# Moving the inverses of norms, their scales and the sums of weights to other slots of the opening of a transformer block

## Chip, cores and metric

The kernel runs on one core of one Trainium2 chip. The metric is the device time of one execution in microseconds; the median of three timed runs is given. Lower is better.

## What is computed

A residual around one transformer block whose norms are conditioned on a vector t. Shapes: x is 4 x 1024 x 512 (four batches of 1024 tokens), t is 4 x 128, 16 heads of 32, hidden size 2048, all float32.

```python
def rmsnorm(x, t, gw, gb, bw, bb):
    g = (t @ gw.T + gb)[:, None, :]
    b = (t @ bw.T + bb)[:, None, :]
    inv_rms = rsqrt(mean(x * x, axis=-1, keepdims=True) + 1e-6)
    return g * x * inv_rms + b

def block(x, t, ...):
    x = x + attention(rmsnorm(x, t, g1w, g1b, b1w, b1b), Wq, Wk, Wv, Wo)
    n = rmsnorm(x, t, g2w, g2b, b2w, b2b)
    return x + (silu(n @ gate_w.T) * (n @ hid_w.T)) @ out_w.T

out = x + block(x, t)
```

The attention is the usual softmax(q k / sqrt(32)) v over the 1024 tokens of a batch, followed by Wo.

## The kernel before

Activations lie with the 512 features over 4 chunks of 128 partitions (C = 4) and the tokens along the free axis. The tokens are cut into 8 blocks of 512 (NBLK = 8), two per batch (QB = 2, called halves). One loop over slots g = 0 to 267 runs everything but the start and the end. In slot g the scores of step r = g are formed: 4 heads, 256 queries, 256 keys. Four steps (UN = 4) make one j, which is one group of 4 heads and 256 queries; eight j (GB = 8), that is 32 slots (BS = 32), make one block of 512 queries. A first slot is one with g % 4 == 0, a second slot one with g % 4 == 1, and so on.

The order of the instructions on TensorE (PE), VectorE (DVE), ScalarE (ACT) and GpSimd (POOL) is written out by hand: each engine runs its instructions in the order of the program, so a late instruction holds up all that stands behind it on its engine. Only the order of SyncE (SP), which issues most DMAs, is left to the framework.

What one slot g of the opening (g below FS = 60) does, in program order:

- scores(g) on PE into the one PSUM tile sc (L337), and in a first slot fold_sum on DVE (L425)
- shifted(g-5) on DVE: the maximum is taken off the raw scores (L390); in a second slot in two halves, since the shift of that j arrives then: parts_T (pt, L374), spread (sp, L113) on PE and two copies on ACT (L385)
- weighted(g-6) on PE (L403), which needs the exponential that ACT made in the slot before; its sum over keys goes by an accumulating DMA from POOL (L417)
- keep(g) on ACT: copies the scores from PSUM (L344)
- exponential(g-5) on ACT (L393), which needs shifted(g-5)
- a projection (project_kq, project_v or project_out) on PE from a queue of chains; its result is copied by ACT to a staging tile and stored to DRAM, or, for project_out, added on DVE (L471). In even slots a second one follows, whose copy comes in the next slot
- in a first slot sums on PE (L435, over the folded tile), the running maximum (L352) and the transposes of the maxima (mt, L358) with parts on DVE (L364 to L369); in the other slots two running maxima (L349)
- what is filed under halfway (by between), then divide, which in a third slot, and for the last j of a block in a first slot, inverts and normalizes an earlier j (L443, L452), then what is filed under ended (by after)

The projections of batches 1 to 3 need their normed inputs y. For each half-batch (b, half) a slot s4 is worked out: 6, 14, 22, 30, 38 and 46, always a third slot. The chunk is loaded in slot s4-7 (L256); norm_squares runs at the end of s4-5 and s4-4 (ACT L139, DVE L142 and L145); norm_root in s4-3 (one product and a square root on ACT, L150, with loads of the activation table); the inverse at the end of s4-2 (L746, 128x512); the four norm_scale in s4 (DVE L200), one for each chunk c; the norm_mod on ACT (L203) at the end of s4 for c = 0, 1 and of s4+1 for c = 2, 3. The projections that use it start at s4+6.

The feed-forward stage from slot 60 on multiplies 2x2 blocks with sums of weights. These sums are made in the opening by weight_sums, for f = 0 to 15: step 0 issues two loads of 256 KB on SP (L495), step 1 does four DVE operations on 128x256 (L501 to L504) and issues two stores (L506). Its four tiles and the staging tiles of the projections share the tag h with seven buffers. Step 1 of f is at the end of slot 3f+6: slots 6, 9, 12 and so on to 51.

At the end of slots 47 and 48 the squares of the first feed-forward norm, f0, are formed (L139, L142, L145), and its mean in slot 49.

Of the kernel before, what the change touches and what calls it, by code (L numbers as in the profile page):

```python
# [24 lines left out]
def tile_cond_transformer_block(  # L25
# [13 lines left out]
    nc = tc.nc  # L39
# [77 lines left out]
    y, wkq, wv, wo, kq, v = {}, {}, {}, {}, {}, {}  # L117
# [3 lines left out]
    state = {}  # L121
# [13 lines left out]
    def norm_squares(dst, tag: str, k: int):  # L135

        sq = [sb.tile([P, NB], F32, tag="t", name=f"sq{tag}_{2 * k + i}", bufs=2) for i in range(2)]
        for i in range(2):
            nc.scalar.activation(sq[i], dst[:, 2 * k + i, :], AF.Square)  # L139
        if k == 0:  # L140
            state[tag] = sb.tile([P, NB], F32, tag="tot", name=f"tot{tag}", bufs=1)
            nc.vector.tensor_tensor(state[tag], sq[0], sq[1], ALU.add)  # L142
        else:
            for t in sq:
                nc.vector.tensor_tensor(state[tag], state[tag], t, ALU.add)  # L145
# [53 lines left out]
    def norm_scale(dst, tag: str, c: int):  # L199
        nc.vector.tensor_tensor(dst[:, c, :], dst[:, c, :], state[tag], ALU.mult)  # L200

    def norm_mod(which: int, b: int, dst, c: int):
        nc.scalar.activation(  # L203
            dst[:, c, :],
            dst[:, c, :],
            AF.Identity,
            bias=mod[:, (2 * which + 1) * C + c, b : b + 1],
            scale=mod[:, 2 * which * C + c, b : b + 1],
        )
# [498 lines left out]
    def pin(g, fn, *a):  # L708
        pinned.setdefault(g, []).append((fn, a))

    def between(g, fn, *a):
        halfway.setdefault(g, []).append((fn, a))

    def after(g, fn, *a):
        ended.setdefault(g, []).append((fn, a))

    def chains_of(b: int, half: int):
        todo = []
        for hg in range(C):
            todo.append(((load_wkq, (hg,)), project_kq, (b, hg, 0, half)))  # L720
            todo.append((None, project_kq, (b, hg, 1, half)))
        for kt in range(half * KT // 2, (half + 1) * KT // 2):
            todo.append((None, project_v, (b, kt)))
        return todo

    def enqueue(g: int, load, fn, a):
        queue.append((g, load, fn, a))
# [9 lines left out]
    for b in range(1, B):  # L737
        for half in range(QB):
            s = math.ceil((len(queue) + 1) / PACE)
            s4 = s - 4 - (s - 6) % UN  # L740
            tag = f"a{b}_{half}"
            pin(max(s4 - 7, 0), load_y, b, half)
            for k in range(2):
                after(s4 - 5 + k, lambda b=b, half=half, tag=tag, k=k: norm_squares(y[b, half], tag, k))
            between(s4 - 3, norm_root, tag)
            after(s4 - 2, lambda tag=tag: nc.vector.reciprocal(state[tag], state[tag]))  # L746
            for c in range(C):
                between(s4, lambda b=b, half=half, tag=tag, c=c: norm_scale(y[b, half], tag, c))
                after(s4 + c // 2, lambda b=b, half=half, c=c: norm_mod(0, b, y[b, half], c))
            for load, fn, a in chains_of(b, half):  # L750
                enqueue(s, load, fn, a)
    FS = BS + 28
    for f in range(NF):
        after(3 * f + 4, weight_sums, f, 0)
        after(3 * f + 6, weight_sums, f, 1)
    for n in range(NBLK):
        g0 = (n + 1) * BS
        pin(g0 + 6, load_res, n)
# [5 lines left out]
        if n < NBLK - 1:  # L764
            tag = f"f{n}"
# [46 lines left out]
    with tc.manual_schedule(  # L812
# [51 lines left out]
        g = 0  # L864
# [309 lines left out]
```

## Time and profile before

| what | us |
| --- | --- |
| median of three timed runs (2425.57 to 2426.95) | 2425.66 |
| the profiled execution | 2425.87 |
| its span, first to last instruction | 2424.1 |
| busy in the span: PE | 2374.3 |
| busy in the span: DVE | 1975.1 |
| busy in the span: ACT | 1420.1 |
| busy in the span: POOL | 172.4 |
| start, 0 to 44.49 | 44.49 |
| opening, slots 0 to 59 | 476.55 |
| attention and feed-forward, 521.04 to 2143 | 1621.96 |
| the rest of the feed-forward | 281.10 |

The mean granted clock of TensorE is 0.998. A row of the timeline gives the start and the duration in us, the engine, the line of the kernel, the operation, the tiles (written from read), the shapes and how many were merged; a bracket at its end is the time that the engine stood idle just before, and who released it. PE's ends are modelled, and successive rows overlap by about 0.1 us, so a cost in a chain is read from the start of one row to the start of the next.

The six long inverses take this much each (minimum, median and maximum in ns, then the first and last start):

```profile
L746 DVE RECIPROCAL tota<-tota x6: 3344/3346/3346, 79.7 to 402.6; 128x512 f32<-128x512 f32 x6
```

### The profile page before, as it was taken

How to read it: one execution, taken by the hardware profiler on the slowest of the kernel's cores; microseconds unless marked ns; L12 is line 12 of the kernel's file. 1: busy time of each engine (PE TensorE's matmuls, PEld its weight loads, DVE VectorE, ACT ScalarE, POOL GpSimd, SP SyncE). 2: the span in 40 equal slices, each digit the busy share in tenths (PEclk: the TensorE clock that was granted, in tenths of full speed). 3: DMA queues.
4: the chain of work that ended last, by engine and by line, in shares of the span. 5: the costliest groups of instructions: out<-in, count | busy, mean ns of one | idle time of the engine just before them, and what ended most of it. 6: DMA issues, size and time to landing. Idle time of an engine off the chain costs nothing. (4 is left out here: it accounts for less than half of the span.)

```text
span 2424.1 us, 74021 instructions
## 1 busy us (share of the span) xinstructions
PE 2374.3 (98%) x33149; PEld 1153.2 (48%) x33149; DVE 1975.1 (81%) x2295; ACT 1420.1 (59%) x1519; POOL 172.4 (7%) x207
## 2 busy tenths in 40 slices
PE   9999999999999999999999999999999999989999
PEld 4333434345454544544454545454545454434665
DVE  2688888889799988998899979997999799835544
ACT  4677776766566656665576657665666576412111
POOL 0000000000000000000000000000000000000000
PEclk9999999999999999999999999999999999999999
DMA  6699999889888888889888888898887988862331
GB/s 226 188 295 254 262 251 241 222 220 239 199 203 212 204 226 199 216 212 229 196 211 217 221 201 213 202 238 202 206 210 197 231 197 219 209 213 82 126 106 53
DMA packets 184843, 499.79 MB, mean 206 GB/s; under 512 B 21191, under 2 KB 78535, under 8 KB 157134
## 3 DMA queue, kind: packets, MB, share of 16 engines
q0 software_dynamic: 28656, 208.68, 44.4%
q1 hardware_dynamic: 155582, 286.37, 35.0%
q8 instruction: 261, 4.28, 0.7%
q14 instruction: 56, 0.46, 0.1%
q10 hardware_dynamic: 288, 0.01, 0.0%
HBM read 244.34 MB, written 41.97 MB: 118 GB/s over the span
## 5 line engine op out<-in xcount | busy, mean ns | idle before, releaser
L390 DVE TENSOR_TENSOR raw<-raw,shift 128x2048 f32<-128x2048 f32 (+1 forms) x320 | 588.8, 1857 | 26.1 <-ACT shift L385 26.1
L344 ACT COPY raw<-sc 128x2048 f32<-128x2048 f32 x256 | 479.4, 1873 | 186.2 <-PE sc L337 127.8
L393 ACT ACTIVATE raw<-raw 128x2048 f32<-128x2048 f32 x256 | 490.7, 1917 | 147.5 <-DVE raw L390 145.3
L349 DVE TENSOR_TENSOR rmax<-rmax,raw 128x1024 f32<-128x1024 f32 x384 | 469.5, 1223 | 47.6 <-ACT raw L344 41.0
L113 PE MATMUL pc<-h,ow 128*32 128x512 f32 x3328 | 379.9, 595 | 2.5 <-ACT raw L393 1.5
L417 POOL DMA_DIRECT2D raw<-raw x192 | 165.3, 861 | 1940.7 <-ACT raw L393 839.0
L337 PE MATMUL sc<-q,k 32*128 32x256 f32 x4096 | 293.3, 400 | 0.8 <-ACT raw L344 0.8
L403 PE MATMUL av<-raw,v 128*32 128x256 f32 x4096 | 272.5, 384 | 21.3 <-ACT raw L393 20.8
L113 PE MATMUL pa<-x,fa 128*32 128x256 f32 x4096 | 270.0, 381 | 3.5 <-DVE pa L551 2.5
L113 PE MATMUL pa<-sums,fw 128*32 128x256 f32 x4096 | 267.9, 379 | 0.0
L337 PEld LDWEIGHTS sc<-q,k 32*128 32x128 f32 x4096 | 185.0, 184 | 117.1 <-issue 74.9
L113 PE MATMUL pkq<-y,wkq 128*32 128x512 f32 (+1 forms) x1664 | 230.8, 596 | 0.9 <-ACT y L203 0.7
L113 PEld LDWEIGHTS pc<-h,ow 128*32 128x32 f32 x3328 | 103.7, 110 | 206.9 <-issue 193.0
L113 PEld LDWEIGHTS pa<-x,fa 128*32 128x32 f32 x4096 | 123.3, 110 | 112.1 <-DVE pa L551 20.9
L113 PEld LDWEIGHTS pa<-sums,fw 128*32 128x32 f32 x4096 | 133.1, 110 | 87.9
L403 PEld LDWEIGHTS av<-raw,v 128*32 128x32 f32 x4096 | 110.6, 109 | 134.5 <-ACT raw L393 48.7
L113 PE MATMUL pb<-x,fw 128*32 128x256 f32 x2048 | 134.7, 379 | 1.2 <-ACT pb L566 1.2
L113 PE MATMUL pa<-x,fw 128*32 128x256 f32 x2048 | 134.0, 379 | 0.0
L113 PE MATMUL pb<-sums,fa 128*32 128x256 f32 x2048 | 133.9, 379 | 0.0
L583 ACT ACTIVATE t<-pa 128x512 f32<-128x512 f32 x128 | 78.3, 612 | 92.9 <-PE pa L113 92.6
L113 PEld LDWEIGHTS pkq<-y,wkq 128*32 128x32 f32 (+1 forms) x1664 | 72.6, 117 | 125.3 <-issue 117.4
L385 ACT COPY shift<-sp 128x512 f32<-128x512 f32 x128 | 75.0, 586 | 95.0 <-PE sp L113 95.0
(132 smaller groups left out, 2338.2 us busy)
## 6 DMA issues: line engine op xcount, KB each, us to landing
raw<-raw POOLq DMA_DIRECT2D x192, 1024.0 KB, 9.2
fw<-sw SPq DMA_DIRECT2D x128, 512.0 KB, 7.3
fa<-in_gh_w SPq DMA_DIRECT2D x128, 384.0 KB, 6.1
ow<-in_out_w SPq DMA_DIRECT2D x104, 256.0 KB, 3.6
wkq<-in_kq_w SPq DMA_DIRECT2D x32, 512.0 KB, 5.8
v<-vs SPq DMA_DIRECT2D x128, 128.0 KB, 6.4
k<-kqs SPq DMA_DIRECT2D x124, 128.0 KB, 6.8
kqs<-st SPq DMA_DIRECT2D x61, 256.0 KB, 8.0
```

Of the source, the lines that this page charges most:

```text
L113: nc.tensor.matmul(dst[k : k + n, :], w[:, k : k + n], moving, start=start, stop=stop, skip_group_check=seeded)
L337: nc.tensor.matmul(sc[:, i, k, :], keys[rows, k * P : (k + 1) * P], queries[rows, :], start=True, stop=True)
L344: nc.scalar.copy(raw[r].rearrange("p k h q -> p h k q"), state.pop(("sc", r)))
L349: nc.vector.tensor_tensor(rmax[j], rmax[j], raw[r][:, k, :, :], ALU.max)
L385: nc.scalar.copy(shift[j][:, k : k + 2, :], pp)
L390: nc.vector.tensor_tensor(t, t, s.unsqueeze(1).to_broadcast(list(t.shape)), ALU.add)
L393: nc.scalar.activation(raw[r], raw[r], AF.Exp)
L403: nc.tensor.matmul(av[j][i * DH : (i + 1) * DH, :], v[m, u][:, k, i * DH : (i + 1) * DH], raw[r][:, k, i, :], start=(kt == 0), stop=(kt == ...
L417: nc.gpsimd.dma_start(out=acc[j].rearrange("p k h q -> p (k h q)"), in_=raw[r].rearrange("p k h q -> p (k h q)"), accum_op=ALU.add,)
L583: nc.scalar.activation(state["t", p], bank_a[p], AF.Tanh, scale=0.5)
```

## The change

Three things in the schedule of the opening. The inverse of each norm goes from the end of slot s4-2 (a first slot) to the end of slot s4-1 (a second slot). Of the four scales, c = 0, 1 stay in s4 and c = 2, 3 go to s4+1. The sums of weights are filed in groups of three to each eight slots: step 1 of f is at slot g = 8 (f // 3) + 2 (f % 3) + 7, which is 7, 9, 11, 15, 17, 19, 23, 25, 27, 31, 33, 35, 39, 41, 43 and 47, and step 0 two slots earlier. In the terms of the norms these are slots s4+1, s4+3 and s4+5, the last of which is s4-3 of the next half-batch.

```diff
             between(s4 - 3, norm_root, tag)
-            after(s4 - 2, lambda tag=tag: nc.vector.reciprocal(state[tag], state[tag]))
+            after(s4 - 1, lambda tag=tag: nc.vector.reciprocal(state[tag], state[tag]))
             for c in range(C):
-                between(s4, lambda b=b, half=half, tag=tag, c=c: norm_scale(y[b, half], tag, c))
+                between(s4 + c // 2, lambda b=b, half=half, tag=tag, c=c: norm_scale(y[b, half], tag, c))
                 after(s4 + c // 2, lambda b=b, half=half, c=c: norm_mod(0, b, y[b, half], c))
...
     for f in range(NF):
-        after(3 * f + 4, weight_sums, f, 0)
-        after(3 * f + 6, weight_sums, f, 1)
+
+        g = 8 * (f // 3) + 2 * (f % 3) + 7
+        after(g - 2, weight_sums, f, 0)
+        after(g, weight_sums, f, 1)
```

## The prediction

> **What bounds the kernel now.** I read the page first, then the busy time by stage, the waits of the opening, and the engines' rows in order of time. A slot is one pass of the loop over g; it begins with its scores product (L337). Slots 0 to 59 are the opening, 44.49 to 521.04 us. The chain of waits covers only the end, from about 2206 us, so it says nothing of the opening.
>
> ```profile
> 44.49:521.04 476.55, 465.03 (x4885) 187.12 (x4884) 389.66 (x406) 340.85 (x346) 35.47 (x42) 1.00 0.90 240
> ```
>
> The columns are the stretch, its length and the busy time of PE, PEld, DVE, ACT and POOL. PE lacks only 476.55 - 465.03 = 11.5 us, more than which cannot be won by removing waits. What these waits are:
>
> ```profile
> ACT raw L393 <- DVE raw L390: 44.8, 31, 3.1
> ...
> PE av L403 <- ACT raw L393: 9.0, 9, 1.6
> ```
>
> Nine waits, 9.0 us: the weighted product of slot g (L403) needs the exponential of slot g-1 (L393), which needs that slot's subtraction on DVE (L390). DVE works in order, so whatever stands ahead of L390 on DVE reaches PE once the slack is used up. Two of the nine:
>
> ```profile
> 200.51 1.07 PE L403 MATMUL av<-raw,v 128*32 128x256 f32 x16 [0.60 <-ACT raw L393]
> ...
> 232.42 0.85 PE L403 MATMUL av<-raw,v 128*32 128x256 f32 x12 [0.68 <-ACT raw L393]
> ```
>
> These are slots 20 and 24. The others: slot 6 0.86, 12 1.13, 14 1.57, 32 0.67, 36 0.59, 38 1.57, 48 1.34; besides, slots 22, 30 and 46 lose about 0.1 each. From slot 49 to 59 no wait of PE is shown, so time lost or won before slot 49 passes to the end whole. The DVE chain behind the wait of slot 24 (slot 21 begins at 210.05, slot 24 at 230.60):
>
> ```profile
> 209.67 3.35 DVE L746 RECIPROCAL tota<-tota 128x512 f32<-128x512 f32 x1
> 212.93 2.29 DVE L390 TENSOR_TENSOR raw<-raw,shift 128x1024 f32<-128x1024 f32 x2
> 215.14 2.48 DVE L349 TENSOR_TENSOR rmax<-rmax,raw 128x1024 f32<-128x1024 f32 x2
> 217.53 0.42 DVE L501 TENSOR_TENSOR s<-gh 128x256 f32<-128x256 f32 x1
> ...
> 219.00 2.29 DVE L390 TENSOR_TENSOR raw<-raw,shift 128x2048 f32<-128x2048 f32 x1
> 221.21 2.48 DVE L349 TENSOR_TENSOR rmax<-rmax,raw 128x1024 f32<-128x1024 f32 x2
> 223.60 2.49 DVE L200 TENSOR_TENSOR y<-y,tota 128x512 f32<-128x512 f32 x4
> 226.01 1.75 DVE L443 RECIPROCAL total<-total 128x256 f32<-128x256 f32 x1
> ...
> 228.13 2.29 DVE L390 TENSOR_TENSOR raw<-raw,shift 128x2048 f32<-128x2048 f32 x1
> ```
>
> The reader sees that the long reciprocal (L746) fills time in which DVE must wait anyway: at 213 us the second half of slot 21's shift is only just there (ACT copies it until 213.25). From then on DVE has no gap until the product of slot 24 waits. From the start of one row to the next: reciprocal 3.26, sums of weights 1.47, subtraction 2.21, maxima 2.39, four scales 2.41, L443 with L452 2.12; from the last L390 to the product 232.42 - 228.13 = 4.29.
>
> **The change part by part.** No instruction is added or removed; 6 reciprocals, 24 scales and 16 sets of weight sums move, with 32 loads and 32 stores of 256 KB on SP.
>
> *Reciprocal from the end of slot s4-2 to that of s4-1, scales c=2,3 from s4 to s4+1.* The chain s4-1 to s4+2 gets 3.26 more and, ahead of its last L390, 1.20 less. No sums of weights lie in slots s4-1 or s4 any more.
> - Slots 14 and 38: today reciprocal (3.35) and sums both end slots 12 and 36 and push the halves of slot 13 from about 147 to 149.09. That goes: -1.57 twice, and the three waits of 0.1: -3.4.
> - Slots 24 and 32 have sums in the chain today (ends of slots 21 and 30): +3.26 - 1.47 - 1.20 = +0.59 each, +1.2.
> - Slots 16 and 40 have no wait today, PE having stood two slots before. An undelayed second slot (slot 25, from 241.96) ends its maxima 7.40 after its start. 7.40 + 3.26 + 2.21 + 2.39 + 1.20 + 2.12 + 4.29 = 22.87; the product is due at 5.92 + 9.01 + 5.51 + 1.07 = 21.51 (slots 17, 18, 15, scores). Wait 1.35 each, +2.7.
> - Slot 8: L425, L443 and L452 don't run before slot 12, the chain is over 3 us shorter, 0.
>
> Behind the scales on ACT are the modulations of c=2,3, then the copy of the scores (L344), which sc and mt wait for: by the same sums it ends at 27.6 after slot 13's start, mt is due at 27.7. Covered, barely.
>
> *Sums of weights.* Those at s4+1 (f = 0, 3, 6, 9, 12) come before the fold (L425) and the subtraction of the first slot, whose DVE then idles until mt (L352 shows 1.7 to 4.4 us of it). With the later chain: 18.58 (last L390) + 2.20 + 2.40 + 1.20 + 1.47 + 1.14 + 2.20 = 29.19, against 28.93 at which L352 could start after mt. So pt (L374) waits 0.2 in slots 17, 25, 33, 41: +0.8. Those at s4-3 (f = 2, 5, 8, 11, 14) hide in that idle time; without it, 1.47 each. Those at s4+3 (f = 1, 4, 7, 10, 13) lie in the chain to slots 12, 20, 28, 36, 44. Slots 12, 20 and 36 have a set there now, no change. Slot 28 has none: its L390 at 259.29 becomes 260.76, plus 4.29 is 265.05 against 264.37: +0.7. The chain to slot 44 holds no L443 and has its set already, 0.
>
> *Slot 48* is the dearest place. Its fold is the last of a long row on DVE, just in time for the product over it:
>
> ```profile
> 429.09 1.22 DVE L425 TENSOR_TENSOR raw<-raw 128x1024 f32<-128x1024 f32 x1
> ...
> 430.41 0.64 PE L435 MATMUL sum<-raw,ones_sum 128*32 128x256 f32 x8
> ```
>
> The chain adds about 0.5 (3.26 - 1.47 - 1.20, less 0.1 from halves that start on time), so L403 waits 1.85 in place of 1.34. Then slot 47 takes two scales (1.20) and f=15 (1.47), both ahead of the fold. On ACT the last modulation, hence both squares of the norm f0 (L139), wait for the scales: 428.08 + 1.2 ends the scales, modulation to 430.2, squares to 431.4, their sum on DVE (L142) to 432.1, fold to 433.3. The product is due at 426.56 + 0.89 + 3.47 = 430.92: it waits 2.4, and pt 0.1 more. +3.0. Before's trace has no such wait: the bounds are 0 (fold in time) and 2.5 (all 3.2 of added DVE work less the 0.84 idle ahead of L142, and ACT's delay); I take 2.4, as every term of it is a row.
>
> *SP and the buffers.* Up to seven tiles of the tag h are in use. In a run of three sets, two loads, two sums and three staging copies come every two slots, seven in all, so a staging copy reuses the third before it, 13.7 us or more later (225.75, 212.06). Stores kqs<-st land in 8.1, at most 10.8 us. I take 0. The nearest row of a wait is 0.51 (ACT L286 at 128.87, for a store); one per slot group would be 3 us, the upper bound; below nothing is excluded, as no PE wait on a DMA exists to be removed. The stores of sums hold SP until DVE is done (14 waits, 32.8 us, longest 5.1); behind them are loads of keys, queries and values and the staging stores. A key load of slot 14 (150.91) landed at 160.2 for scores at 166.82: 6.6 spare. 0.
>
> **Sum:** -3.4 + 1.2 + 2.7 + 0.8 + 0.7 + 3.0 = +5.0. The profiled execution took 2425.87 (span 2424.1 and 1.8 around it), 0.2 above the median 2425.66. 2425.87 + 5.0 = 2430.9.
>
> **The clock.** Long waits have a second price here:
>
> ```profile
> 130.50:133.91 3.41, 1.50 (x24) 0.99 (x28) 3.38 (x4) 3.02 (x3) 0.00 (x0) 1.00 1.06 246
> 133.91:137.32 3.41, 3.41 (x28) 1.11 (x24) 3.38 (x3) 3.38 (x4) 0.00 (x0) 0.50 1.01 276
> ```
>
> PE idled 1.91 of 3.41 us and the next 3.41 ran at granted clock 0.50: L403 took 1.66 for 1.07, the product after it 4.79 for 3.62, together 1.8 us lost. 1.57 idle (slot 14) did not do it. The 2.4 of slot 48 can, depending on where the stretch of 3.41 falls. The Trainium skill (TensorE: Matmul & The Clock Gate, HAM oscillation) asks only that no idle gap exceed some 3.4 us; by that rule slot 48 costs nothing more, by the row up to 1.8. The row stands against the rule, for gaps shorter than the window sufficed.
>
> **Rivals.** (1) The same with one clock drop in slot 48: 2430.9 + 1.8 = 2432.7. For it: 2.4 is above 1.91. Against: it may split over two stretches. (2) Not slower: the fold of slot 48 is in time, as the modulation order or idle time absorbs it; 2430.9 - 2.4 = 2428.5. It decides where L435 waits under about 2 us. Against: in-order ACT and DVE. (3) Faster: the moved reciprocal is absorbed in every chain and all waits but those of slots 6 and 12 go: 2425.87 - 7.5 = 2418.4. For it: DVE is idle 18% of the opening; against: the rows above are gapless just where it is put. (4) The burst of sums starves the staging buffers or SP: with 3 us, 2433.9, more if keys come late. For it: DMA share 0.90 over the opening; against: landing times.
>
> **How the numbers follow.** A measurement of this kernel tells about 0.2% (4.85 us) from no change. Forecast 0.45, by itself 2429.3 to 2432.0, of it 0.28 past the bound of 2430.5; (1) 0.20, (2) 0.17, (3) 0.06, (4) 0.12. Slower 0.28 + 0.20 + 0.12 = 0.60, same 0.17 + 0.17 = 0.34, faster 0.06. The range from 2427.0 to 2434.5 leaves out (3), the low end of (2) and the worst of (4).
>
> **What would show it.** L403 waiting near 1.3 in slots 16, 24, 32, 40 and none in 14 and 38; 0.6 to 0.7 in slots 20, 28, 36; L435 waiting over 2 us in slot 48, with its fold after L142; pt waits of 0.2 in slots 17, 25, 33, 41. I am wrong if slot 16 has no wait, if the fold of slot 48 starts before its product is due, or if ACT's L286 waits for stores.

## The result, and the profile after

| | before | changed |
| --- | --- | --- |
| median, us (lowest to highest, 6 runs each) | 2425.61 (2423.93 to 2426.95) | 2435.11 (2431.22 to 2436.95) |
| profiled execution, us | 2425.87 | 2435.64 |
| its span, us | 2424.1 | 2433.8 |

The ratio is 1.0038, with a 95% interval from 1.0027 to 1.0049: slower, by more than the 0.2% that can be told from no change, and 4.2 us above the forecast of 2430.9 us, outside its range.

The opening by the same two views as before, from slot 0 to slot 60. First the busy time of PE, PEld, DVE, ACT and POOL in the stretch:

```profile
44.37:528.70 484.33, 467.28 (x4886) 186.80 (x4885) 390.59 (x406) 339.18 (x346) 35.41 (x41) 0.99 0.88 236
```

It is 484.33 - 476.55 = 7.8 us longer. PE lacks 484.33 - 467.28 = 17.05 us where it lacked 11.5; the other 2.2 is longer time of the same matmuls, at a mean clock of 0.99 for 1.00. The waits of the opening (who waited for what, us in total, times, longest):

```profile
ACT raw L393 <- DVE raw L390: 63.1, 31, 4.5
...
PE av L403 <- ACT raw L393: 9.9, 10, 1.9
...
PE pkq L113 <- DMA wkq<-in_kq_w: 4.4, 1, 4.4
```

The exponential waits for the subtraction 63.1 us where it waited 44.8, yet the sum of the waits of L403 goes up by 0.9 only: one sort of wait moved from slots 14 and 38 to slots 16 and 40. The last row is new. Before, no wait of PE on a DMA stood in the opening; now one product of a projection waits 4.45 us for its weights. It is in slot 10, in PE's rows in order of time (start, duration, releaser of the idle time before):

```profile
119.18 1.07 PE L403 MATMUL av<-raw,v 128*32 128x256 f32 x16
124.70 8.60 PE L113 MATMUL pkq<-y,wkq 128*32 128x512 f32 x64 [4.45 <-DMA wkq<-in_kq_w]
```

The same two rows in the kernel before:

```profile
119.24 1.07 PE L403 MATMUL av<-raw,v 128*32 128x256 f32 x16
120.13 7.05 PE L113 MATMUL pkq<-y,wkq 128*32 128x512 f32 x64
```

Before, the product began 0.89 after the start of L403 and took 7.05. Now it begins 5.52 after it, 4.63 later, and takes 1.55 longer: 6.2 us in one slot. The stretches of 3.41 us around it say why it is longer (columns as above; the last three are granted clock, DMA share, GB/s):

```profile
121.01:124.42 3.41, 0.00 (x0) 0.00 (x0) 3.38 (x6) 1.19 (x1) 0.00 (x0) 1.00 1.01 266
124.42:127.83 3.41, 3.13 (x16) 0.79 (x20) 2.77 (x3) 1.91 (x1) 0.76 (x1) 0.50 1.03 404
```

PE does nothing in the first, and the second runs at clock 0.50. The DMA share is full in both.

Slot by slot, against before, the 9.7 us of span are these (the start takes 0.1 less):

| slots | forecast | measured | what is seen |
| --- | --- | --- | --- |
| 10 to 12 | 0 | +3.0 | slot 10 +6.19; slots 11 and 12 give back 1.04 and 2.17 |
| 13 to 47 | +2.0 | +1.8 | 14 and 38 -1.5 each; 16 and 40 +1.5, 24 and 32 +0.75, 28 +0.66; 20 and 36 as before |
| 48 | +3.0 | +2.9 | L403 waits 1.85, L435 0.55, clock 0.50 for 3.41 us |
| 68 | 0 | +0.6 | a product waits 2.13 for a DMA of out weights, before 1.53 (put down to ACT there) |
| after the last slot | 0 | +1.5 | clock 0.50 for 6.83 us instead of 3.41 |

The give-back in slots 11 and 12: PE stood so long in slot 10 that DVE and ACT caught up; the waits of 0.16 and 0.80 us before slot 12 and the clock drop at 133.91 are gone.

The DVE chain to slot 24, for comparison with the one shown before:

```profile
215.06 2.36 DVE L390 TENSOR_TENSOR raw<-raw,shift 128x1024 f32<-128x1024 f32 x2 [2.42 <-ACT shift L385]
217.91 2.48 DVE L349 TENSOR_TENSOR rmax<-rmax,raw 128x1024 f32<-128x1024 f32 x2 [0.49 <-ACT raw L344]
220.32 3.34 DVE L746 RECIPROCAL tota<-tota 128x512 f32<-128x512 f32 x1
...
228.11 1.28 DVE L200 TENSOR_TENSOR y<-y,tota 128x512 f32<-128x512 f32 x2
...
231.44 2.28 DVE L390 TENSOR_TENSOR raw<-raw,shift 128x2048 f32<-128x2048 f32 x1
```

DVE now idles 2.42 us ahead of the first half of the subtraction, where the reciprocal used to stand, and the reciprocal lies in the part without gaps; the scales are two, not four. The last L390 starts at 231.44 and PE's row says what that makes:

```profile
235.72 1.07 PE L403 MATMUL av<-raw,v 128*32 128x256 f32 x16 [1.18 <-ACT raw L393]
```

The forecast had 235.73 by its own rule (last L390 plus 4.29) and a wait of 1.27 here (0.68 + 0.59); it is 1.18.

### The profile page after: what moved, and what is told of

It reads as the page before. It is cut to its first block, busy times and chain, and to the rows that moved or that the text cites. A ratio compares the mean times of both kernels' runs of the same rounds, so it can differ in the third digit from the quotient of the medians.

```text
span 2433.8 us, 74014 instructions
## 1 busy us (share of the span) xinstructions
PE 2378.0 (98%) x33149; PEld 1152.2 (47%) x33149; DVE 1975.6 (81%) x2295; ACT 1419.1 (58%) x1519; POOL 172.5 (7%) x207
## 5 line engine op out<-in xcount | busy, mean ns | idle before, releaser
L390 DVE TENSOR_TENSOR raw<-raw,shift 128x2048 f32<-128x2048 f32 (+1 forms) x320 | 588.4, 1855 | 42.9 <-ACT shift L385 42.9
L403 PE MATMUL av<-raw,v 128*32 128x256 f32 x4096 | 272.6, 384 | 22.4 <-ACT raw L393 22.0
L403 PEld LDWEIGHTS av<-raw,v 128*32 128x32 f32 x4096 | 110.5, 109 | 136.1 <-ACT raw L393 51.5
```

What stands on the lines that cost most here:

```text
L390: nc.vector.tensor_tensor(t, t, s.unsqueeze(1).to_broadcast(list(t.shape)), ALU.add)
L403: nc.tensor.matmul(av[j][i * DH : (i + 1) * DH, :], v[m, u][:, k, i * DH : (i + 1) * DH], raw[r][:, k, i, :], start=(kt == 0), stop=(kt == ...
```

## The experiments

All are edits of one of the two kernels, timed against the kernel before on the same chip; its median was 2426.25 (21 runs), 2425.64 (27) and 2425.71 (23) in the three sets. d(49) is the start of slot 49 less that of the kernel before, which gathers everything up to it; a part of d(49) between -1.1 and +0.9 lies ahead of slot 10, at the very start, and is named where it matters.

### Which sums make PE wait for weights: first_sum_old, first_sum_moved

On SP's queue, before (start, time, what is issued):

```profile
96.31 1.64 SPq L506 DMA_DIRECT2D sw<-s  x2
...
103.36 0.43 SPq L495 DMA_DIRECT2D gh<-in_gh_w  x1
107.38 0.33 SPq L256 DMA_DIRECT2D y<-in_x  x1
108.06 0.68 SPq L287 DMA_DIRECT2D kqs<-st  x1
108.79 3.35 SPq L261 DMA_DIRECT2D wkq<-in_kq_w  x2
```

and in the changed kernel:

```profile
104.21 2.72 SPq L506 DMA_DIRECT2D sw<-s  x2
106.98 1.27 SPq L495 DMA_DIRECT2D gh<-in_gh_w  x1
108.30 1.21 SPq L256 DMA_DIRECT2D y<-in_x  x1
109.61 1.26 SPq L287 DMA_DIRECT2D kqs<-st  x1
110.92 2.02 SPq L261 DMA_DIRECT2D wkq<-in_kq_w  x2
```

The stores of f = 0 and the second load of f = 1 have moved from 96 and 103 us to just ahead of the load of the chunk y (1024 KB) and of the two loads of weights (512 KB each). Before, the first load of weights, issued at 108.79, landed 10.7 us later, at 119.5, for a product at 120.13: 0.6 us to spare.

```profile
DMA to landing us min/median/max: 10.7/10.7/10.7
```

In the changed kernel it is issued at 110.92, 2.1 us later, and the product that waits for it starts 13.8 us after that. So some 2 us are lost ahead of the issue, on SP's queue, and some 3 behind it, in the transfer. The first pair puts f = 0 alone back into the changed kernel, and moves f = 0 alone in the kernel before.

```diff
         g = 8 * (f // 3) + 2 * (f % 3) + 7
+        g = 6 if f == 0 else g
```

> The whole change, but the sums of f=0 stay as before (loads at the end of slot 4, sums and stores at the end of slot 6). Theory A (the wait of 4.45 us for a weight load wkq in slot 10 comes from the loads and stores of f=0, which now stand directly ahead of the input load and two wkq loads): no PE wait on a DMA in slot 10, so 3.0 us less than the changed kernel in slots 10 to 12; what is left are the DVE chains, +1.8 in slots 13 to 47 and +2.9 in slot 48, together about +4.7, 2430.3. Theory B (the wait comes from the grouping of the later sums, or of the inputs' timing): the wait stays, about +7.7 in the opening. Theory C (the clock takes the time): slots 13 to 48 differ between the two kernels.

```diff
-        after(3 * f + 4, weight_sums, f, 0)
-        after(3 * f + 6, weight_sums, f, 1)
+        after(3 * f + (5 if f == 0 else 4), weight_sums, f, 0)
+        after(3 * f + (7 if f == 0 else 6), weight_sums, f, 1)
```

> The kernel before, with only the sums of f=0 one slot later (loads at the end of slot 5, sums and stores at the end of slot 7). Theory A: a PE wait for wkq of 3 to 5 us appears in slot 10, and nothing else changes from slot 14 on: +3, with +1 to +4 for how it meets the waits of slots 11 and 12; 2428.6. Theory B: no wait, 2425.6. On DVE the move costs nothing under either theory.

first_sum_moved: 2428.67 us, ratio 1.0014 (1.0005 to 1.0023). With nothing but f = 0 one slot later, the wait is there. The weights' load in this kernel (time from issue to landing), issued at 109.23, and the product:

```profile
DMA to landing us min/median/max: 14.3/14.3/14.3
```

```profile
123.58 8.77 PE L113 MATMUL pkq<-y,wkq 128*32 128x512 f32 x64 [3.11 <-DMA wkq<-in_kq_w]
```

109.23 + 14.3 = 123.53, and the product starts at 123.58. Issued 0.4 us later than before, the load needs 14.3 us instead of 10.7: most of the delay is in the transfer. Slots 11 and 12 give back 3.2 here too; d(49) is +2.0.

first_sum_old: 2434.84, ratio 1.0032 (1.0020 to 1.0045). The wait at the first product of slot 10 is gone, but the second product waits 2.08, so the theory that f = 0 alone is behind it falls in part. Slots 10 to 12 together are +0.8 instead of +3.0. What was won there was lost in slot 48: L435 waits 2.24 and a clock drop follows it, +4.36 in all, where the changed kernel has +2.9. Put back alone, f = 0 therefore brings back little time.

### The rest of the wait: three_first_old, third_sum_moved, no_sums_ahead

The second product's wait was put down to the third set, f = 2, which the change makes one slot earlier. The first of these puts three sets back into the changed kernel, the second moves the third set alone in the kernel before.

```diff
         g = 8 * (f // 3) + 2 * (f % 3) + 7
+        g = 3 * f + 6 if f < 3 else g
```

> The whole change, but the sums of f=0, 1 and 2 stay in the slots of before (6, 9, 12). With f=0 alone put back, a PE wait for wkq of 2.1 us was left in slot 10. Theory A2 (the DMA engines are full from 96 to 130 us and the wkq loads of slot 10 land with almost nothing to spare, so that any transfer of the sums that is moved into that stretch, f=0's stores or f=2's loads, makes them late): no PE wait on wkq, the opening costs the DVE chains alone, +4.7; 2431 and d(slot 60) = +4.7. Rival (the moved inverse delays the first accumulating DMA of POOL by 2.7 us, and this is what collides): the wait of 2 us stays, d(slot 60) = +7 or more.

```diff
-        after(3 * f + 4, weight_sums, f, 0)
-        after(3 * f + 6, weight_sums, f, 1)
+        early = 1 if f == 2 else 0
+        after(3 * f + 4 - early, weight_sums, f, 0)
+        after(3 * f + 6 - early, weight_sums, f, 1)
```

> The kernel before, with only the sums of f=2 one slot earlier (loads at the end of slot 9, sums at the end of slot 11). Theory A2: a PE wait for wkq of about 2 us in the second product of slot 10, and with the sums gone from slot 12 the wait of slot 14 (1.57) goes: net about 0 (-2 to +2), 2426. Rival: no wait in slot 10, -1.6; 2424.

In both the theory missed, and the wait came out as the rival had it. three_first_old (2431.23, ratio 1.0024, 1.0015 to 1.0033) still has 2.00 us of wait at the second product, though without a clock drop, so that slots 10 to 12 are -1.0 in sum. That its time is the theory's 2431 is luck: d(49) is +5.2, with 1.4 more than expected in slot 48. third_sum_moved (2423.79, ratio 0.9994, 0.9985 to 1.0003) has none at all. The sums of f = 2 are not the cause. No load of f = 0 to 2 differs between three_first_old and the kernel before, so what is left must come with the moved inverse and scales. But neither the kernel with the moved inverse alone nor that with the moved scales alone (both below) has such a wait. Each of these traces shows one execution, so whether it takes both moves or varies from one execution to the next can't be told. This rest of 2 us stays open. One candidate, not tried alone, is POOL's accumulating transfer of 1024 KB, issued at 114.52 in three_first_old and at 117.48 before; against it, it is at 114.37 in that kernel with the moved inverse.

The next test is of the amount of data itself: the changed kernel, with f = 0 and f = 1 at slots 51 and 53, so that 1 MB of loads and stores no longer lies ahead of the weights.

```diff
         g = 8 * (f // 3) + 2 * (f % 3) + 7
+        g = 51 + 2 * f if f < 2 else g
```

> The whole change, but the sums of f=0 and f=1 go to the ends of slots 51 and 53, loads two slots earlier: 2 MB of loads and stores less around the wkq loads, of which the loads of f=1 and the stores of f=0 (1 MB) stood directly ahead of them. Theory A2 (backlog of the DMA engines): no PE wait for wkq in slot 10, neither at its first product (4.45 us in the changed kernel) nor at its second (2.0 us with f=0 put back); d(slot 49) about +4 to +5, of which slot 48 +2.9 or +4.4. Rival (the wait comes from when the input y is loaded or from POOL's transfer alone, not from the amount ahead): 2 us or more of wait stay.

2429.19 us, ratio 1.0020 (1.0010 to 1.0029). The product of slot 10 waits for nothing and runs at full clock:

```profile
121.01 7.05 PE L113 MATMUL pkq<-y,wkq 128*32 128x512 f32 x64
```

With those transfers gone the whole wait is gone, the rest of 2 us too: it needs the backlog of the sums' transfers, though for the rest that alone isn't enough, as the kernel before has the loads and stores of f = 0 and 1 and no wait. The first load of weights, issued at 109.91 here, is there within 11.1 us, where the product that waits for it in the changed kernel starts 13.8 us after the issue. From slot 14 to slot 49 this kernel loses 4.8 us with no clock drop among them, which is the change's price on DVE and ACT alone; the forecast's terms for it summed to +5.0. Slots 11 and 12 give 3.2 (the sums that stood ahead of them are gone), and 0.9 is lost at the very start.

### The parts alone: sums_alone, inverse_alone, scales_alone

```diff
-        after(3 * f + 4, weight_sums, f, 0)
-        after(3 * f + 6, weight_sums, f, 1)
+        g = 8 * (f // 3) + 2 * (f % 3) + 7
+        after(g - 2, weight_sums, f, 0)
+        after(g, weight_sums, f, 1)
```

> Only the sums of weights are moved, inverses and scales stay as before. By the DVE chains: the waits of slots 14 and 38 (1.57 each), 24, 32 (0.68, 0.67) and 48 (1.34) go, slot 28 gets 0.6, so -5.0 from slot 13 on; with the wait for wkq in slot 10 +3.0: 2423.6. Rival: the inverse at the end of a first slot delays the halves whatever follows it, so slots 14 and 38 keep about 1 us each: -3 from slot 13 on, 2425.6.

2423.76, ratio 0.9991 (0.9983 to 1.0000). The wait for weights in slot 10 is there, 4.17 us. From slot 14 to 49 the kernel gains 4.6 (expected 5.0): slots 14 and 38 lose their waits (-1.46 each), 24 and 32 theirs (-0.74), slot 48 0.92, and slot 28 gets one (+0.68). The sums in second and fourth slots are therefore a gain on DVE; their cost is on the DMA queues.

```diff
-            after(s4 - 2, lambda tag=tag: nc.vector.reciprocal(state[tag], state[tag]))
+            after(s4 - 1, lambda tag=tag: nc.vector.reciprocal(state[tag], state[tag]))
```

> Only the inverses are moved to the end of the second slots. By the DVE chains each s4-1 to s4+2 chain gets the whole 3.26 with nothing taken out: waits of about 2.4 in slots 16 and 40, 3.4 to 3.9 in slots 24, 32 and 48, and slots 14 and 38 lose theirs: +11 to +12, 2437; no wait for wkq in slot 10. Rival: the inverse fills a gap of DVE in the second slots too, so only the 1.57 of slots 14 and 38 changes: 2422.5.

2446.72, ratio 1.0083 (1.0070 to 1.0097): the dearest part. Three of the products that wait:

```profile
168.57 1.07 PE L403 MATMUL av<-raw,v 128*32 128x256 f32 x16 [2.39 <-ACT raw L393]
...
304.63 1.94 PE L403 MATMUL av<-raw,v 128*32 128x256 f32 x16 [3.85 <-ACT raw L393]
...
372.26 1.93 PE L403 MATMUL av<-raw,v 128*32 128x256 f32 x16 [2.39 <-ACT raw L393]
```

d(49) is +18.1, above the 11 to 12 that waits alone would give. Most of the rest is the clock, about 7 us in slots 24, 32, 40 and 48; new waits make slots 8, 23 and 47 longer by 2.8 together. On the clock: slot 16 (first row) costs 2.46 and slot 40 (last row) 4.14 with the very same wait, because the product of slot 40 runs at clock 0.50 (1.93 for 1.07) and so does what follows it.

```diff
-                between(s4, lambda b=b, half=half, tag=tag, c=c: norm_scale(y[b, half], tag, c))
+                between(s4 + c // 2, lambda b=b, half=half, tag=tag, c=c: norm_scale(y[b, half], tag, c))
```

> Only the scales c=2,3 are moved to slot s4+1. By the DVE chains 1.20 us leave the chains to slots 24, 32 and 48: waits 0.68 and 0.67 go, that of L403 in slot 48 falls from 1.34 to 0.2, but the last modulation and the squares behind it come later, so L435 there waits 1.5 to 2; slots 14, 20, 36 and 38 as before: -0.5 to -0.9, 2425. Rival (the scales are the harmful part): +1 or more.

2426.94, ratio 1.0007 (0.9998 to 1.0016). Slots 24 and 32 lose their waits as expected (-0.74 each). In slot 48 L403 waits 0.14 for 1.34, but L435 then waits 2.23 and a clock drop follows: +2.58. The expected gain is missed by that drop and by the wait of L435, which is above the 1.5 to 2 expected here and near the forecast's 2.4.

### Slot 48: last_sum_old

The forecast charged slot 48 to two things at once, ACT's chain (scale, modulation, squares of f0, fold) and the sums of f = 15 ahead of the fold. Here those sums go back to slot 51.

```diff
         g = 8 * (f // 3) + 2 * (f % 3) + 7
+        g = 51 if f == 15 else g
```

> The whole change, but the sums of f=15 are at the end of slot 51 in place of 47. Theory A (slot 48 is set by ACT: last scale, last modulation, two squares, their sum, fold): L435 still waits and slot 48 is as long as with the change, 15.2 us, for the sums of weights only fill DVE's wait for the squares; same time as the changed kernel. Rival (slot 48 is set by DVE's own work): slot 48 is 1.5 us shorter, 13.7.

2437.04, ratio 1.0046 (1.0032 to 1.0060). L435 still waits 2.24, so the sums hide behind ACT's chain and cost nothing there. That chain in the changed kernel:

```profile
432.83 1.28 DVE L200 TENSOR_TENSOR y<-y,tota 128x512 f32<-128x512 f32 x2
...
433.55 1.52 ACT L203 ACTIVATE y<-y,mod 128x512 f32<-128x512 f32 x2 [2.27 <-DVE y L200]
...
434.98 1.13 ACT L139 ACTIVATE sqf<-x 128x512 f32<-128x512 f32 x2
...
436.14 0.69 DVE L142 TENSOR_TENSOR totf<-sqf,sqf 128x512 f32<-128x512 f32 x1 [0.56 <-ACT sqf L139]
...
436.75 1.22 DVE L425 TENSOR_TENSOR raw<-raw 128x1024 f32<-128x1024 f32 x1
...
438.07 0.64 PE L435 MATMUL sum<-raw,ones_sum 128*32 128x256 f32 x8 [0.55 <-issue]
```

ACT waits for the scales, its squares come at 434.98, DVE then waits 0.56 for them with its own sums done, and the fold is last. The idle of 0.55 ahead of L435 is put down to issue, but its fold ends at 437.97, and that is what it waits for. In the changed kernel this wait is short, as PE was slowed first:

```profile
428.21:431.62 3.41, 1.56 (x28) 0.93 (x28) 3.38 (x4) 1.93 (x2) 0.00 (x0) 1.00 0.80 177
431.62:435.03 3.41, 3.41 (x28) 1.16 (x24) 3.38 (x7) 1.48 (x3) 1.72 (x2) 0.50 0.60 115
```

The wait of L403 (1.85) falls into one stretch of 3.41 us, the next runs at half clock, and L403 and the product after it take 1.7 us longer, in time that PE would else have waited. In last_sum_old no drop comes there, though its L403 waits 1.86 in one stretch too; what made the difference isn't shown. The drop comes after L435, and slot 48 is 1.4 us longer for it (+4.36).

### Is there a better order: spread_sums, sums_in_gaps

As the sums alone gained on DVE, the next two keep the inverse and the scales of the kernel before and choose the slots of the sums one by one: f = 0 stays at slot 6, and the others avoid the last slots of each chain.

```diff
-        after(3 * f + 4, weight_sums, f, 0)
-        after(3 * f + 6, weight_sums, f, 1)
+        g = (6, 9, 15, 19, 23, 27, 31, 35, 39, 41, 43, 49, 51, 53, 55, 57)[f]
+        after(g - 2, weight_sums, f, 0)
+        after(g, weight_sums, f, 1)
```

> The kernel before with inverses and scales as before and only the sums of weights moved, to the ends of slots 6, 9, 15, 19, 23, 27, 31, 35, 39, 41, 43, 49, 51, 53, 55, 57, the loads two slots earlier: none of them in a chain that PE waits for, and none of f=2's transfers among the wkq loads of slot 10. By the DVE chains the waits of slots 14, 38 (1.57 each), 20, 36 (0.6 each), 24, 32 (0.68, 0.67) and 48 (1.34) go: -7.0; 2418.6 to 2419.2. Rival (the DMA engines are the bound wherever the sums go): a wait on a DMA appears elsewhere and takes 3 us or more of it.

2426.88, ratio 1.0005 (0.9996 to 1.0014). By slot 59 it is 8.3 us ahead (1.1 of it from the start), the waits of slots 14, 20, 24, 32, 36, 38 and 48 gone. Then L403 of slot 59 waits 3.82 behind the sums at 55 and 57 and a clock drop follows: +5.58. Slot 68 adds 2.2. The second takes other slots:

```diff
+        g = (6, 9, 11, 15, 19, 23, 27, 31, 35, 39, 41, 43, 47, 49, 51, 53)[f]
```

> The kernel before with only the sums of weights moved, to the ends of slots 6, 9, 11, 15, 19, 23, 27, 31, 35, 39, 41, 43, 47, 49, 51, 53, loads two slots earlier: f=0 and 1 as before, none after slot 53 (the sums at 55 and 57 made L403 of slot 59 wait 3.8 us in the kernel with spread sums), none in a chain that PE waits for. By the DVE chains the waits of slots 14, 20, 24, 32, 36, 38 and 48 go and slot 59 has none: -7.0 at slot 60; with the wait for ow in slot 68 as it is, 2418 to 2420, below both kernels. Rival (the DMA engines are the bound): a new wait on a DMA in slot 10 or slot 68 takes 2 us or more of it, 2421 or more.

2417.73 us (2416.70 to 2419.39), ratio 0.9969 (0.9958 to 0.9980): faster than both kernels. From slot 0 to slot 60:

```profile
43.40:513.29 469.89, 464.80 (x4885) 186.97 (x4884) 389.62 (x406) 341.04 (x346) 35.62 (x42) 1.00 0.90 244
```

PE lacks 469.89 - 464.80 = 5.1 us instead of 11.5, with the same 4885 matmuls. By slots it gains 1.46 in 14 and in 38, 0.66 in 20, 0.75 in 24, 0.73 in 32, 0.67 in 36 and 0.94 in 48, together 6.7; 1.1 lies at the start. No product of the opening waits for weights. The three late sums at 49, 51 and 53 cost no wait of PE.

### The kernel before, once more: before_again

> The kernel before once more, to see which of its waits vary. If the wkq loads of slot 10 land with next to nothing to spare, a wait of 0 to 1 us can show there in some executions; the waits of L403 in slots 14 to 48 come from the order on DVE and are the same to 0.1 us. The stretch of halved clock in slot 12 may be missing or elsewhere, which is worth up to 1.8 us.

2429.28 us, 3.6 above the median of its set. All waits of the DVE chains come out as in the first profile, within 0.1. What differs is the start (+0.7), slot 12 (0.27 and 1.66 for 0.80 and 1.13, the same sum), slot 68 (a wait of 2.05 for the out weights and a clock drop, +2.1) and the clock drop after the last slot (6.83 us instead of 3.41). So the +0.6 and the +1.5 that the table gives to slot 68 and to the end are within what the kernel before does by itself; they aren't shown to belong to the change.

## Why the prediction was wrong, and where it held

**The step that failed** is "SP and the buffers", of which it said "I take 0". It looked at the right resource in the wrong places: at the staging stores and at one key load of slot 14 with 6.6 us to spare. The loads that the burst of sums runs into are the weights of slot 10, which had 0.6. Their issue stands right behind the two stores and the load that the change moves, at a time when the DMA engines are full (a share of about 1.0). Rival (4) came nearest, with +3 and the lowest chance but one; the places it named were the staging buffers and SP, and ACT's L286 waits for no store in the changed kernel. None of the three signs by which it would be wrong came up, as none of them looks at these loads. Measured: +6.2 in slot 10 and +3.0 after slots 11 and 12 have caught up. The kernel with f = 0 alone moved has the wait, and the one without the sums ahead has not.

**The DVE chains held.** Waits in slots 16 and 40 are 1.18 (forecast 1.35), in slots 24 and 32 1.18 (1.27), in slot 28 0.59 (0.7), none in 14 and 38, slots 20 and 36 unchanged. L374 waits 0.16 in slots 16, 24, 32 and 40, which the forecast named by the slot after, at 0.2. The sum is +1.8 for +2.0.

**Slot 48 held in size.** L403 waits 1.85, as forecast; the whole slot is +2.90 for +3.0, and +2.91 in the kernel without the sums ahead and without a clock drop, where L435 waits 2.24 for 2.4. The cause was ACT's chain, as worked out; the sums of f = 15 that it also counted did not count.

**Rival (1)**, a clock drop in slot 48, came true and cost nothing in this execution, since it replaced most of the wait of L435. In first_sum_old, three_first_old and last_sum_old the drop came after L435 instead, and slot 48 was +4.36 or +4.37, 1.4 to 1.5 above the case without a drop; the rival had 1.8 for it. Why it came early or late isn't shown: the stretch with the wait of L403 held 1.85 us of idle PE in the one case and 1.86 in the others.

**The rule on the clock.** The prediction weighed the Trainium skill (TensorE: Matmul & The Clock Gate, HAM oscillation), that PE should have no idle gap over some 3.4 us, against a row, and sided with the row. The runs bear that out: gaps of 2.39 and 1.85 us were followed by half clock.

**The sum.** The profiled execution is 4.7 us above the forecast: 3.0 from slot 10, 2.1 from slot 68 and the end, -0.3 from the terms that it had. Only the first of these is shown to be the change's.

## What to carry to other kernels

When transfers are moved on a queue, list each load that is issued within the next ten microseconds or so behind them, and set its landing time against its first use, the tightest first: one load with time to spare says nothing of its neighbour. Slack against a DMA isn't a constant where the DMA engines are full; with only f = 0 moved up close ahead of it, a load issued 0.4 us later landed 4 us later. And a gain on one engine (the sums between the chains) can be had without its cost on another if the few items that collide stay where they were.

## What the runs showed of the hardware

The TensorE clock is granted in stretches of 3.41 us, and what counts first is the idle time inside one of them. In the kernel with the inverse alone moved, half clock begins at 133.36, 235.76, 304.03, 372.30 and 440.56, all whole multiples of 3.413 us apart, which gives the other boundaries. Two waits of 2.39 us end differently there. Slot 16, then slot 40:

```profile
164.08:167.50 3.42, 2.11 (x28) 0.84 (x20) 3.42 (x3) 1.04 (x2) 0.00 (x0) 1.00 0.98 196
167.50:170.91 3.41, 2.34 (x32) 1.07 (x36) 3.34 (x7) 3.41 (x5) 0.86 (x1) 1.00 1.00 354
368.89:372.30 3.41, 1.02 (x20) 0.60 (x22) 3.38 (x3) 2.00 (x2) 0.00 (x0) 1.00 0.97 221
372.30:375.71 3.41, 3.41 (x28) 1.16 (x32) 3.38 (x7) 3.41 (x4) 0.86 (x1) 0.50 1.05 356
```

In slot 16 the boundary at 167.50 cuts the wait in two (1.31 and 1.07 of idle), and the clock stays; in slot 40 the whole wait lies in one stretch, and the next has clock 0.50. Over the traces of this study, from slot 0 on, drops from full clock followed stretches with 1.84 us or more of idle PE (the least in before_again, from 131.27), and none followed one with 1.82 or less (the most in the kernel before, from 2140.95). From 1.85 to 2.08 both happened (2.08 without a drop in inverse_alone, from 604.40), so the idle time alone doesn't decide there. A drop cost 1.4 us in slot 48 and 1.7 in slot 40, or nothing where PE would have had to wait anyway (slot 48, +2.90 with it and +2.91 without). The Trainium skill (TensorE: Matmul & The Clock Gate, What's actually happening) says that the window is free-running and about 3.4 us long, which agrees with these rows and with the boundaries of other traces, which lie elsewhere from the start of the span (133.91 before, 124.42 in the changed kernel, 2.78 stretches apart); that half clock comes after a whole idle window does not.

The other is how steeply a load's landing grows. The first load of 512 KB of weights for slot 10, issued between 107.8 and 109.3 us, landed 9.7 us after issue in the fastest kernel, 9.9 with the inverse alone moved, 10.7 before and 14.3 with f = 0 moved. (The changed kernel's trace has no landing time for it; in last_sum_old, which differs from it by f = 15 alone, the load, issued at 110.20, landed after 14.9.) The DMA share is 0.96 to 1.06 in every 4 us from 96 to 120, before as in the changed kernel, and 0.88 to 1.07 in the kernel without the sums ahead: what queues ahead of a load shows in its landing, not in the share.
